# Turning heads and attention outputs in 32 x 32 blocks on VectorE and by way of DRAM, in the first transformer block

## The chip, the cores and the metric

The kernel runs on one core of a Trainium2 chip. The metric is device time in microseconds. A core has TensorE (PE; its weight loads are shown apart as PEld), VectorE (DVE), ScalarE (ACT), GpSimd (POOL) and SyncE (SP), which here only issues DMAs. Each engine and each queue works through its own list in order. Matrix products land in PSUM, which this part of the kernel uses as eight banks of 128 x 512 float32.

## The reference, cut to what matters

Two transformer blocks follow each other on `x` of 8 batches, 512 rows and 256 columns, all in float32. The change touches only the self attention of the first:

```python
h = modulate(ln(x), shift_sa, scale_sa)
q = ln(_heads(h, H)) * qn_w + qn_b        # 16 heads of 16 columns
k = ln(_heads(h, H)) * kn_w + kn_b
v = _heads(h, H)
attn = softmax(einsum('bhqd,bhkd->bhqk', q, k) * scale)
h = _unheads(einsum('bhqk,bhkd->bhqd', attn, v))
x = x + gate_sa[:, None, :] * h
```

After it the first block has cross attention over 64 context rows and a gated feed-forward layer. The second block has 64 columns a head and rotary positions.

## The kernel before, in words

`x` of a batch lies as 128 partitions by four row tiles (`NT`) by 256 columns. The first block handles one batch after another, and three stages of neighbouring batches are interleaved: `cycle(c)` issues self attention of batch `c` (`sa[c]`), the beginnings of that of `c + 1` (`nxt`), cross attention of `c - 1` (`x`, class `CrossAttention`) and feed-forward of `c - 2` and `c - 3` (`up`, `down`). `beginning()` does batch 0 and `ending()` what is left. The whole order is written by hand (`tc.manual_schedule` over all five engines): each engine issues in the order of the Python text. Which of the eight banks a `bank()` gets (line 75) is chosen by the framework when it builds the program.

The 16 heads are taken in four groups `g` of four heads. `c, par = divmod(g, 2)` picks a half of the columns (`zs[c]`) and even or odd heads, so that heads lie 32 partitions apart after a transpose.

- The heads' own normalisation: `centre` (DVE, L538 to L540), `square` (ACT, L544), `var` (DVE, L550, L551) and `scale` (POOL, the power L557 and the product L558) leave normed rows in `zs[c]`.
- `queries_keys(g)` transposes them: four 128 x 128 transposes on PE (L566) into a bank, then q and k on DVE out of that bank (L569, L570).
- `score(g, kt)` makes the scores of one tile of 128 keys, in four banks, one a head, four matmuls beside each other in the array; `exponentials` empties them on ACT (L615).
- `value(g, kt)` adds up the values of the four tiles of keys in one bank `o`, with the softmax denominators in a 17th column. After the last, ACT copies the bank to the tile `oT` (L591).
- `back(g)`, one group later, transposes `oT` by four PE transposes (L598) into a bank. DVE divides (L605 to L607) and checks (L129), POOL applies the gate and adds to `x` (L609, L610).

`group(scores, beside, short, values, rest)` sets the order of a group: two tiles' scores, `beside`, the other two tiles' scores, `short`, then the values. In a cycle group 0, 1, 2, one group of cross attention and group 3 follow each other. `short` of group 3 holds `nxt.queries_keys(0)`, `x.inverse(1)` (L687), `x.scaled(1)` (L691, L129), `nxt.var(1)` and `nxt.scale(1)`. In the steady cycles (3 to 6) `beside` of groups 0 and 1 ends with `blocks` of the feed-forward and of cross attention: `blocks_turned` (L413 to L418) turns 32 x 32 blocks of the normed rows on DVE, stores them to DRAM by four DMAs on SP and reads them back by one, so that `modulated` (ACT, L427) has them transposed. `spread` (L398) brings a row of gates or shifts to all partitions, on SP too. In cycle 1, `keys1` (matmuls, L868 and L869 on DVE, L873 and L874 on POOL) prepares keys for the second block, and after cycle 1 the feed-forward weights are loaded (L239).

Of the kernel before, what the change touches and what calls it, by code (L numbers as in the profile page):

```python
# [10 lines left out]
F32 = mybir.dt.float32  # L11
I32 = mybir.dt.int32
AF = mybir.ActivationFunctionType
ALU = mybir.AluOpType
# [30 lines left out]
def fast_path(ctx: ExitStack, tc: tile.TileContext, a: dict, out: bass.AP):  # L45

    nc = tc.nc
# [3 lines left out]
    small = ctx.enter_context(tc.tile_pool(name="small", bufs=4))  # L51
    dram = ctx.enter_context(tc.tile_pool(name="dram", bufs=2, space=bass.MemoryType.DRAM))
# [22 lines left out]
    def bank():  # L75
        return psum.tile([P, 512], F32, tag="bank", name="ps_B", bufs=8)
# [10 lines left out]
    def mm(o, lhsT, rhs, start=True, stop=True):  # L87
        nc.tensor.matmul(o, lhsT, rhs, start=start, stop=stop)  # L88


    ident = const.tile([P, P], F32, name="ident")
# [6 lines left out]
    rows = const.tile([P, 5 * D], F32, name="rows")  # L98
# [16 lines left out]
    def col(name):  # L115
        lo, hi = _COLS[name]
        return cols[:, lo:hi]
# [7 lines left out]
    def check(src):  # L125
        c = checks[0]
        checks[0] += 1
        for i, op in enumerate((ALU.max, ALU.min)):
            nc.vector.tensor_reduce(chk[:, i, c : c + 1], src, AX.X, op)  # L129
# [23 lines left out]

    def rstd_of(var, n, eps):

        r = small.tile([P, 64], F32, tag="rstd", name="rstd")
        nc.vector.tensor_scalar_add(r[:, :n], var, eps)  # L157
        nc.gpsimd.tensor_tensor(r[:, :n], r[:, :n], mhalf[:, :n], ALU.pow)  # L158
        return r
# [46 lines left out]
    qk_cols = keep0.tile([P, 2], F32, name="qk_cols")  # L206
# [3 lines left out]
    wk = sa0.enter_context(tc.tile_pool(name="sa0", bufs=2, side="right"))  # L210
# [3 lines left out]
    zs = [wk.tile([P, NT, DZ], F32, name=f"z{c}", bufs=1) for c in range(2)]  # L214
# [181 lines left out]
    def spread(dst, b, lo, n):  # L396

        nc.sync.dma_start(dst, modd[b : b + 1, lo : lo + n].to_broadcast([P, n]))  # L398
# [32 lines left out]
    def normed_in_pieces(pool, b, eps, take):  # L431

        def rows_():
            z = pool.tile([P, NT, D], F32, tag="z", name="z", bufs=1)
            take(z)
            return z

        return norm_pieces(rows_, xs[b], eps)
# [44 lines left out]
    class SelfAttention:  # L483
# [69 lines left out]
        def scale(self, c, par=None, eng=None):  # L553
# [3 lines left out]
            nc.gpsimd.tensor_tensor(var, var, half, ALU.pow)  # L557
            (eng or nc.gpsimd).tensor_tensor(z, z, var[:, :, :, None].to_broadcast([P, NT, n, HD0]), ALU.mult)  # L558

        def queries_keys(self, g):  # L560

            c, par = divmod(g, 2)
            ps = bank()
            lo = par * HD0
            for t in range(NT):
                nc.tensor.transpose(ps[:, t * P : (t + 1) * P], zs[c][:, t, lo : lo + P], ident)  # L566
            q = wk.tile([P, N], F32, tag="q", name="q", bufs=1)
            k = wk.tile([P, N], F32, tag="k", name="k", bufs=1)
            nc.vector.tensor_scalar(q, ps, qk_cols[:, 0:1], qk_cols[:, 1:2], ALU.mult, ALU.add)  # L569
            nc.vector.tensor_scalar(k, ps, col("kw"), col("kb"), ALU.mult, ALU.add)  # L570
            self.s[g] = (q, k)
# [9 lines left out]
        def value(self, g, kt):  # L581
            s = self.s
            c, par = divmod(g, 2)
            if kt == 0:
                s["o", g] = bank()
            for j in range(4):
                mm(s["o", g][32 * j : 32 * j + 32, :], s["h"][:, kt, 8 * c + 2 * j + par, :], s["p", kt][j],
                   kt == 0, kt == NT - 1)
            if kt == NT - 1:
                s["oT", g] = oT = wk.tile([P, N], F32, tag="oT", name="oT", bufs=1)  # L590
                nc.scalar.copy(oT, s["o", g])  # L591

        def back(self, g):
            b, s = self.b, self.s
            c, par = divmod(g, 2)
            ps = bank()
            for t in range(NT):
                nc.tensor.transpose(ps[:, t * P : (t + 1) * P], s["oT", g][:, t * P : (t + 1) * P], ident)  # L598
            attn = wk.tile([P, NT, 4, HD0], F32, tag="attn", name="attn", bufs=1)
            x, gate = (v.rearrange("p t (h d) -> p t h d", d=HD0)[:, :, 8 * c + par : 8 * c + 8 : 2]  # L600
                       for v in (xs[b], s["gate"][:, None, :]))
            i = ps.rearrange("p (t j e) -> p t j e", t=NT, j=4)
            inv = small.tile([P, NT, 4], F32, tag="inv", name="inv")
            den = small.tile([P, NT, 4], F32, tag="den", name="den")
            nc.vector.tensor_copy(den, i[:, :, :, HD0])  # L605
            nc.vector.reciprocal(inv, den)
            nc.vector.tensor_tensor(attn, i[:, :, :, 0:HD0], inv[:, :, :, None].to_broadcast([P, NT, 4, HD0]), ALU.mult)  # L607
            check(inv.rearrange("p t j -> p (t j)"))
            nc.gpsimd.tensor_tensor(attn, attn, gate.to_broadcast([P, NT, 4, HD0]), ALU.mult)  # L609
            nc.gpsimd.tensor_tensor(x, x, attn, ALU.add)  # L610
# [21 lines left out]
    class CrossAttention:  # L632
# [4 lines left out]
        def prepare(self, n):  # L637

            b, s = self.b, self.s
            if n == 0:  # L640
                s["gate"] = gate = wk2.tile([P, D], F32, tag="gate", name="gate", bufs=3)
                spread(gate, b, G_CA, D)
                s["pieces"] = normed_in_pieces(wk2, b, EPS0, lambda z: s.update(z=z))
            s["pieces"][n]()
            if n < 2:
                return
            gate = s["gate"]
            gb = wk2.tile([P, D], F32, tag="gb", name="gb", bufs=1)
            nc.gpsimd.tensor_tensor(gb, gate, row("cab0"), ALU.mult)
            add_row(b, gb)  # L650
# [96 lines left out]
    def group(scores, beside, short, values, rest=()):  # L747

        for fn in (*scores[:2], *beside, *scores[2:], *short, *values, *rest):
            fn()  # L750
# [50 lines left out]
    def cycle(c):  # L801

        s, nxt, prev = sa[c], of(sa, c + 1), sa[c - 1]
        x, done = ca[c - 1], of(ca, c - 2)
        up, down = of(ff, c - 2), of(ff, c - 3)
        keys = [lambda p=p: keys1(p) for p in range(NPAIR)] if c == 1 else [lambda: None] * NPAIR
        store = store_keys1 if c == 1 else lambda g: None
        late = [up.turn] if c == 2 else []
        soon, then = ([x.turn], []) if c == 1 else ([], [x.turn])
        rows2, rows3 = ([] if c < n else [s.blocks] for s, n in ((x, 2), (up, 3)))  # L810

        scores, values = of_self(s, 0)
        group(scores, [keys[0], keys[1], lambda: done.out(0), lambda: done.out(1), lambda: up.prepare(0), lambda: up.prepare(1),
                       lambda: down.down(0), lambda: up.prepare(2), *rows3],
              [lambda: s.queries_keys(1), lambda: prev.back(3), lambda: nxt.norm(0), lambda: nxt.norm(1)], values, late)
        scores, values = of_self(s, 1)
        group(scores, [keys[2], lambda: store(0), lambda: down.down(1), lambda: x.prepare(0), lambda: x.prepare(1),
                       *([up.turn] if c > 2 else []), lambda: up.up(0), lambda: x.prepare(2), keys[3], lambda: up.up(1), *rows2],
              [lambda: s.queries_keys(2), lambda: s.back(0), *soon, lambda: nxt.norm(2)], values)
        scores, values = of_self(s, 2)  # L820
        group(scores, [keys[4], *then, lambda: store(1), lambda: up.up(2), lambda: up.up(3), lambda: x.queries(0), lambda: x.queries(1)],
              [lambda: s.queries_keys(3), lambda: s.back(1), lambda: nxt.centre(0)], values)
        group([lambda: x.score(0), lambda: x.score(1)],
              [keys[5], lambda: nxt.square(0), lambda: up.up(4), keys[6], lambda: up.up(5), lambda: s.back(2), lambda: nxt.var(0),
               lambda: nxt.scale(0), lambda: nxt.centre(1)], [], [lambda: x.value(0), lambda: x.value(1)])
        scores, values = of_self(s, 3)
        group(scores, [keys[7], lambda: store(2), lambda: x.inverse(0), lambda: up.up(6), lambda: x.scaled(0), lambda: nxt.square(1),
                       lambda: up.up(7)],
              [lambda: nxt.queries_keys(0), lambda: x.inverse(1), lambda: x.scaled(1), lambda: nxt.var(1), lambda: nxt.scale(1)],
              values)  # L830
        store(3)
# [71 lines left out]
    wk2 = wk3 = w_1 = w_3 = w_2 = None  # L903
# [89 lines left out]
    with tc.tile_pool(name="ph4", bufs=2, reuse_waits="tile") as wk:  # L993
        NG = H // 4
        kb, vb = kv_first()
# [1334 lines left out]
```

## Time and profile before

| | us |
|---|---|
| median of 3 runs (2279.99 to 2281.34) | 2280.68 |
| the profiled execution's own time | 2284.83 |
| its span | 2282.9 |
| PE busy | 2258.7 |
| DVE busy | 1143.3 |
| ACT busy | 865.0 |
| POOL busy | 884.0 |
| one steady cycle of the first block (352.90 to 442.06) | 89.16 |

The first block takes about the first 740 us of the span, the second the rest. The line of an instruction is that of the listing above, except that all matmuls of the helper `mm` have L88; a matmul in float32 is recorded as two, a transpose as one. In a timeline row the columns are start, length from first to last instruction of the row, engine, line, operation, written tile and read tiles, and in brackets how long the engine sat idle before it and what ended that. In a row of windows they are the stretch, its length, each engine's busy time (and instructions), the granted PE clock, the DMA engines' busy share and GB/s. Normed heads are `z`, the value bank is a `ps_B` read into `oT`.

### The profile page before, as it was taken

To read this page: it belongs to the slowest core of one execution; us is meant where nothing else is said; L and a number is where in the kernel's file an instruction comes from. 1 tells how busy PE (TensorE), PEld (TensorE's weight loads), DVE (VectorE), ACT (ScalarE), POOL (GpSimd) and SP (SyncE) were. 2 spreads that over 40 slices of the span, in tenths; PEclk is the share of its full clock that TensorE was granted. 3 is DMA by queue.
4 is the path that set the end of the run, shared out by engine and by line. 5 is a ranking of instruction groups with operands and counts; after the bars stand their busy time and mean duration, and the time that the engine had idled before them with its cause. 6 is when DMAs were issued, how large, how long until landed. Compare 5 with 4: busy or idle time off the path is not lost.

```text
span 2282.9 us, 30663 instructions
## 1 busy us (share of the span) xinstructions
PE 2258.7 (99%) x12092; PEld 1139.7 (50%) x12092; DVE 1143.3 (50%) x1978; ACT 865.0 (38%) x1309; POOL 884.0 (39%) x552
## 2 busy tenths in 40 slices
PE   9999999999999999999999999999999999999999
PEld 4444554544545643535353534344445456567666
DVE  5676666665555345353544444444444566643220
ACT  4666555555542133242424243333342131321222
POOL 4653333333200056464645555555544333310110
PEclk9999999999999999999999999999999999999999
DMA  6120110101102001010101010111132445442221
GB/s 194 34 95 22 49 29 21 49 9 41 44 10 77 19 15 39 20 39 20 38 20 39 20 38 20 33 25 31 28 89 79 113 100 128 90 102 52 56 63 36
DMA packets 118119, 115.65 MB, mean 51 GB/s; under 512 B 37600, under 2 KB 91600, under 8 KB 117968
## 3 DMA queue, kind: packets, MB, share of 16 engines
q1 hardware_dynamic: 117104, 111.00, 19.0%
q8 instruction: 97, 1.59, 0.3%
q0 software_dynamic: 576, 2.10, 0.2%
q10 hardware_dynamic: 288, 0.52, 0.1%
q14 instruction: 54, 0.44, 0.1%
HBM read 85.73 MB, written 27.86 MB: 50 GB/s over the span
## 4 chain that ended last, share of the span: by engine, by line
PE 93%; DVE 2%; DMA 2%; POOL 1%; issue 1%; SPq 0%; ACT 0%; DVEq 0%; POOLq 0%; ACTq 0%
PE ps_P L88 41%; PE ps_B L88 30%; PE ps_X L88 7%; PE ps_S L88 6%; PE ps_D L88 5%; PE ps_O L88 3%; DMA rb<-rec 1%; PE ps_B L566 1%; POOL var L557 1%; PE ps_B L598 1%; DVE z L191 0%; DVE p L1337 0%; DMA rec<-rec 0%; DVE t L869 0%; DMA turned_d<-hT 0%
## 5 line engine op out<-in xcount | busy, mean ns | idle before, releaser
L615 ACT ACTIVATE p<-ps_B 128x512 f32<-128x512 f32 x576 | 290.9, 625 | 156.7 <-PE ps_B L88 156.7
L1060 ACT ACTIVATE p<-ps_P 128x1024 f32<-128x1024 f32 x256 | 244.8, 1025 | 87.6 <-PE ps_P L88 87.6
L88 PE MATMUL ps_P<-q,k 32*128 32x512 f32 x2048 | 238.9, 600 | 1.4 <-DVE t L1039 1.4
L1069 POOL TENSOR_TENSOR sm<-sm,p 128x1024 f32<-128x1024 f32 x64 | 177.5, 2774 | 134.8 <-ACT p L1060 134.1
L88 PE MATMUL ps_B<-hT,w 128*128 128x512 f32 x512 | 227.0, 597 | 1.3 <-ACT hT L407 0.9
L88 PE MATMUL ps_P<-p,v 128*32 128x512 f32 x2048 | 226.4, 594 | 0.0
L1028 ACT COPY v<-ps_P 128x1024 f32<-128x1024 f32 x32 | 32.4, 1012 | 377.1 <-PE ps_P L88 377.1
L1069 DVE TENSOR_TENSOR sm<-sm,p 128x1024 f32<-128x1024 f32 x64 | 102.7, 1605 | 144.4 <-ACT p L1060 144.4
L158 POOL TENSOR_TENSOR rstd<-rstd,mhalf 128x4 f32<-128x4 f32 x49 | 52.4, 1069 | 308.7 <-DVE rstd L157 307.5
L88 PEld LDWEIGHTS ps_P<-q,k 32*128 32x128 f32 x2048 | 99.1, 184 | 139.2 <-issue 113.6
L88 PEld LDWEIGHTS ps_B<-hT,w 128*128 128x128 f32 x512 | 95.3, 190 | 127.5 <-issue 97.0
L88 PEld LDWEIGHTS ps_P<-p,v 128*32 128x32 f32 x2048 | 63.3, 110 | 158.3 <-issue 134.0
L88 PE MATMUL ps_B<-q,k 16*128 16x512 f32 x1024 | 140.5, 618 | 1.2 <-DVE k L570 1.2
L1067 POOL TENSOR_TENSOR sm<-p 128x1024 f32<-128x1024 f32 x32 | 79.2, 2474 | 152.6 <-ACT p L1060 152.6
L1038 DVE TENSOR_TENSOR t<-ps_P,rope_c 128x1024 f32<-128x1024 f32 x64 | 78.4, 1225 | 106.7 <-POOL q L1042 64.5
L557 POOL TENSOR_TENSOR var<-var,mhalf 128x32 f32<-128x32 f32 (+1 forms) x17 | 88.0, 5174 | 105.4 <-DVE var L551 105.4
L1067 DVE TENSOR_TENSOR sm<-p 128x1024 f32<-128x1024 f32 x32 | 39.2, 1225 | 171.8 <-ACT p L1060 171.8
L88 PE MATMUL ps_P<-hT,w_sa_wq 128*128 128x512 f32 x256 | 118.4, 605 | 0.8 <-issue 0.8
L88 PE MATMUL ps_B<-p,h 128*32 128x512 f32 x1024 | 118.0, 599 | 0.0
L88 PE MATMUL ps_P<-hT,w_sa_wk 128*128 128x512 f32 x256 | 115.1, 592 | 0.0
L88 PE MATMUL ps_P<-w_sa_wv,hT 128*128 128x512 f32 x256 | 114.9, 592 | 0.0
L873 POOL TENSOR_TENSOR q<-t 128x512 f32<-128x512 f32 x36 | 46.2, 1283 | 177.0 <-DVE t L869 149.7
(245 smaller groups left out, 3660.8 us busy)
## 6 DMA issues: line engine op xcount, KB each, us to landing
z<-turned_d SPq DMA_DIRECT2D x35, 512.0 KB
rb<-rec_d SPq DMA_DIRECT2D x64, 256.0 KB
rb<-rec SPq DMA_DIRECT2D x32, 512.0 KB
turned_d<-hT SPq DMA_DIRECT2D x104, 128.0 KB
turned_d<-sm SPq DMA_DIRECT2D x36, 128.0 KB
out_dram<-x SPq DMA_DIRECT2D x15, 256.0 KB
x<-in_x_dram SPq DMA_DIRECT2D x7, 512.0 KB
gate<-modd SPq DMA_DIRECT2D x24, 128.0 KB
```

Of the source, the lines that this page charges most:

```text
L88: nc.tensor.matmul(o, lhsT, rhs, start=start, stop=stop)
L158: nc.gpsimd.tensor_tensor(r[:, :n], r[:, :n], mhalf[:, :n], ALU.pow)
L557: nc.gpsimd.tensor_tensor(var, var, half, ALU.pow)
L566: nc.tensor.transpose(ps[:, t * P : (t + 1) * P], zs[c][:, t, lo : lo + P], ident)
L598: nc.tensor.transpose(ps[:, t * P : (t + 1) * P], s["oT", g][:, t * P : (t + 1) * P], ident)
L615: nc.scalar.activation(p[i], ps, AF.Exp, scale=HD0 ** -0.5)
L873: nc.gpsimd.tensor_tensor(d[0], ec, os, ALU.subtract)
L1028: nc.scalar.copy(s["v", half][:, t0 : t0 + 2, :], ps)
L1038: nc.vector.tensor_tensor(c, ps, rope_c[:, None, :].to_broadcast([P, 2, N]), ALU.mult)
L1060: nc.scalar.activation(pr, pss[u], AF.Exp, scale=HD1 ** -0.5)
L1067: eng.tensor_tensor(s["sm", g, u], s["p", g, 0, u], s["p", g, 1, u], ALU.add)
L1069: eng.tensor_tensor(s["sm", g, u], s["sm", g, u], s["p", g, kt, u], ALU.add)
```

## The change

In batches 1 to 7 most of these transposes leave PE.

- `heads_turned(c)` is new. DVE turns the 32 x 32 blocks of `zs[c]` into a tile `zt`, four DMAs store it to DRAM, one reads 128 rows back over `zs[c]` (heads of even `g`) and one reads 112 rows into `zt` (odd `g`). `queries_keys` makes q and k from these tiles in SBUF. It is called for `c = 1` at the beginning of group 1's `beside` for the batch itself, and for `c = 0` of the next batch beside cross attention. Batch 0, and groups 0 and 1 of batch 1, keep the PE transposes.
- Where `by_blocks(g)` holds (all of batches 1 to 7 but the last group of batch 7), `value` ends with DVE turning the bank `o` into `oT`, four DMAs to DRAM and one back, in place of ACT's copy. `back` then reads `oT` in SBUF and issues no transpose.
- `centre(0)`, `square(0)`, `var(0)` and `scale(0)` of the next batch move from the cross attention's group to group 2.
- Two tiles get smaller: `rstd` from 64 columns to 4, and the gate of cross attention from three buffers to two.

```diff
+        def heads_turned(self, c):
+            zt = wk.tile([P, N], F32, tag="zt", name="zt", bufs=1)
+            z = zs[c][:, :, 0 : D // 2]
+            nc.vector.transpose(zt.rearrange("p (q t i) -> p t q i", q=4, t=NT), z.rearrange("p t (q j) -> p t q j", j=32))
+            d = dram.tile([4, 32, 4, P], F32, tag="heads", name="heads_d")
+            for r in range(4):
+                nc.sync.dma_start(d[:, :, r, :].rearrange("a j c -> j a c"),
+                                  zt[32 * r : 32 * r + 32].rearrange("j (a c) -> j a c", a=4))
+            d = d.rearrange("a j r c -> (a j) (r c)")
+            raw = zs[c].rearrange("p t d -> p (t d)")[:, 0:N]
+            nc.sync.dma_start(raw, d)
+            nc.sync.dma_start(zt[0 : P - HD0], d[HD0:P])
+            self.s["rows", 2 * c], self.s["rows", 2 * c + 1] = raw, zt[0 : P - HD0]
+
         def queries_keys(self, g):
             c, par = divmod(g, 2)
+            if ("rows", g) in self.s:
+                raw = self.s["rows", g]
+                n = raw.shape[0]
...
+                raw = raw.rearrange("p (r t i) -> p t r i", r=4, t=NT)
+                for o, w, b in ((q, qk_cols[0:n, 0:1], qk_cols[0:n, 1:2]), (k, col("kw")[0:n], col("kb")[0:n])):
+                    nc.vector.tensor_scalar(o[0:n].rearrange("p (t r i) -> p t r i", r=4, t=NT), raw, w, b, ALU.mult, ALU.add)
...
                 s["oT", g] = oT = wk.tile([P, N], F32, tag="oT", name="oT", bufs=1)
-                nc.scalar.copy(oT, s["o", g])
+                if self.by_blocks(g):
+                    nc.vector.transpose(oT.rearrange("p (r t d) -> p t r d", r=4, t=NT),
+                                        s["o", g].rearrange("p (t r i) -> p t r i", r=4, t=NT))
+                    d = dram.tile([4, 32, 4, P], F32, tag="back", name="back_d")
+                    for j in range(4):
+                        nc.sync.dma_start(d[:, :, j, :].rearrange("r i c -> i r c"),
+                                          oT[32 * j : 32 * j + 32].rearrange("i (r c) -> i r c", r=4))
+                    nc.sync.dma_start(oT, d.rearrange("r i j c -> (r i) (j c)"))
+                else:
+                    nc.scalar.copy(oT, s["o", g])
+
+        def by_blocks(self, g):
+            return self.b > 0 and (self.b, g) != (B - 1, 3)
 
         def back(self, g):
-            ps = bank()
-            for t in range(NT):
-                nc.tensor.transpose(ps[:, t * P : (t + 1) * P], s["oT", g][:, t * P : (t + 1) * P], ident)
+            if self.by_blocks(g):
+                i = s["oT", g].rearrange("p (j t e) -> p t j e", t=NT, j=4)
+            else:
+                ps = bank()
+                for t in range(NT):
+                    nc.tensor.transpose(ps[:, t * P : (t + 1) * P], s["oT", g][:, t * P : (t + 1) * P], ident)
+                i = ps.rearrange("p (t j e) -> p t j e", t=NT, j=4)
...
-        group(scores, [keys[2], lambda: store(0), lambda: down.down(1), lambda: x.prepare(0), lambda: x.prepare(1),
+        group(scores, [keys[2], lambda: store(0), lambda: s.heads_turned(1), lambda: down.down(1), lambda: x.prepare(0),
...
-              [lambda: s.queries_keys(3), lambda: s.back(1), lambda: nxt.centre(0)], values)
+        group(scores, [keys[4], *then, lambda: store(1), lambda: up.up(2), lambda: nxt.centre(0), lambda: up.up(3),
+                       lambda: nxt.square(0), lambda: x.queries(0), lambda: x.queries(1)],
+              [lambda: s.queries_keys(3), lambda: s.back(1), lambda: nxt.var(0), lambda: nxt.scale(0)], values)
         group([lambda: x.score(0), lambda: x.score(1)],
-              [keys[5], lambda: nxt.square(0), lambda: up.up(4), keys[6], lambda: up.up(5), lambda: s.back(2), lambda: nxt.var(0),
-               lambda: nxt.scale(0), lambda: nxt.centre(1)], [], [lambda: x.value(0), lambda: x.value(1)])
+              [keys[5], lambda: up.up(4), keys[6], lambda: up.up(5), lambda: s.back(2), lambda: nxt.heads_turned(0),
+               lambda: nxt.centre(1)], [], [lambda: x.value(0), lambda: x.value(1)])
```

More of the change, by code (lines that the diff above doesn't have):

```diff
@@ L154, in rstd_of @@
     def rstd_of(var, n, eps):
-        r = small.tile([P, 64], F32, tag="rstd", name="rstd")
+        r = small.tile([P, NT], F32, tag="rstd", name="rstd")
         nc.vector.tensor_scalar_add(r[:, :n], var, eps)
@@ L558, in scale @@
             (eng or nc.gpsimd).tensor_tensor(z, z, var[:, :, :, None].to_broadcast([P, NT, n, HD0]), ALU.mult)
+        def heads_turned(self, c):
[11 more added lines that the diff above has]
+            self.s["rows", 2 * c], self.s["rows", 2 * c + 1] = raw, zt[0 : P - HD0]
         def queries_keys(self, g):
             c, par = divmod(g, 2)
+            if ("rows", g) in self.s:
+                raw = self.s["rows", g]
+                n = raw.shape[0]
+                q = wk.tile([P, N], F32, tag="q", name="q", bufs=1)
+                k = wk.tile([P, N], F32, tag="k", name="k", bufs=1)
+                raw = raw.rearrange("p (r t i) -> p t r i", r=4, t=NT)
+                for o, w, b in ((q, qk_cols[0:n, 0:1], qk_cols[0:n, 1:2]), (k, col("kw")[0:n], col("kb")[0:n])):
+                    nc.vector.tensor_scalar(o[0:n].rearrange("p (t r i) -> p t r i", r=4, t=NT), raw, w, b, ALU.mult, ALU.add)
+                self.s[g] = (q, k)
+                return
             ps = bank()
@@ L601, in back @@
                        for v in (xs[b], s["gate"][:, None, :]))
-            i = ps.rearrange("p (t j e) -> p t j e", t=NT, j=4)
             inv = small.tile([P, NT, 4], F32, tag="inv", name="inv")
@@ L640, in prepare @@
             if n == 0:
-                s["gate"] = gate = wk2.tile([P, D], F32, tag="gate", name="gate", bufs=3)
+                s["gate"] = gate = wk2.tile([P, D], F32, tag="gate", name="gate")
                 spread(gate, b, G_CA, D)
@@ L816, in cycle @@
         scores, values = of_self(s, 1)
-        group(scores, [keys[2], lambda: store(0), lambda: down.down(1), lambda: x.prepare(0), lambda: x.prepare(1),
-                       *([up.turn] if c > 2 else []), lambda: up.up(0), lambda: x.prepare(2), keys[3], lambda: up.up(1), *rows2],
+        group(scores, [keys[2], lambda: store(0), lambda: s.heads_turned(1), lambda: down.down(1), lambda: x.prepare(0),
+                       lambda: x.prepare(1), *([up.turn] if c > 2 else []), lambda: up.up(0), lambda: x.prepare(2), keys[3],
+                       lambda: up.up(1), *rows2],
               [lambda: s.queries_keys(2), lambda: s.back(0), *soon, lambda: nxt.norm(2)], values)
         scores, values = of_self(s, 2)
-        group(scores, [keys[4], *then, lambda: store(1), lambda: up.up(2), lambda: up.up(3), lambda: x.queries(0), lambda: x.queries(1)],
-              [lambda: s.queries_keys(3), lambda: s.back(1), lambda: nxt.centre(0)], values)
+        group(scores, [keys[4], *then, lambda: store(1), lambda: up.up(2), lambda: nxt.centre(0), lambda: up.up(3),
+                       lambda: nxt.square(0), lambda: x.queries(0), lambda: x.queries(1)],
+              [lambda: s.queries_keys(3), lambda: s.back(1), lambda: nxt.var(0), lambda: nxt.scale(0)], values)
         group([lambda: x.score(0), lambda: x.score(1)],
-              [keys[5], lambda: nxt.square(0), lambda: up.up(4), keys[6], lambda: up.up(5), lambda: s.back(2), lambda: nxt.var(0),
-               lambda: nxt.scale(0), lambda: nxt.centre(1)], [], [lambda: x.value(0), lambda: x.value(1)])
+              [keys[5], lambda: up.up(4), keys[6], lambda: up.up(5), lambda: s.back(2), lambda: nxt.heads_turned(0),
+               lambda: nxt.centre(1)], [], [lambda: x.value(0), lambda: x.value(1)])
         scores, values = of_self(s, 3)
```

## The prediction, made before the result was known

> **What bounds the kernel now.** First the page's busy list, its chain, and the windows of two steady cycles of the first block (one cycle is what `cycle(c)` issues).
>
> ```profile
> PE 2258.7 (99%) x12092; PEld 1139.7 (50%) x12092; DVE 1143.3 (50%) x1978; ACT 865.0 (38%) x1309; POOL 884.0 (39%) x552
> PE 93%; DVE 2%; DMA 2%; POOL 1%; issue 1%; SPq 0%; ACT 0%; DVEq 0%; POOLq 0%; ACTq 0%
> 352.90:442.06 89.16, 89.16 (x492) 44.71 (x496) 55.55 (x114) 49.40 (x95) 29.58 (x19) 1.00 0.12 32
> ```
>
> TensorE is the chain, and in a steady cycle it is busy for all of the 89.16 us; DVE has 33 us to spare. So removing PE work looks like pure gain. But a busy PE is not a PE at its peak, so next I read the PE and ACT timelines at the end of a group of heads.
>
> ```profile
> 368.82 2.03 PE L88 MATMUL ps_B<-q,k 16*128 16x512 f32 x16
> 370.79 0.66 PE L566 MATMUL ps_B<-ident,z 128*128 128x128 f32 x4
> 371.28 0.60 PE L598 MATMUL ps_B<-ident,oT 128*128 128x128 f32 x4
> 371.81 3.64 PE L88 MATMUL ps_B<-p,h 128*32 128x512 f32 x32
> 375.38 2.00 PE L88 MATMUL ps_B<-q,kb 32*128 32x512 f32 x16
> 370.04 4.03 ACT L615 ACTIVATE p<-ps_B 128x512 f32<-128x512 f32 x8 [5.66 <-PE ps_B L88]
> ```
>
> Two sets of four transposes take 371.81 - 370.79 = 1.02 us, 0.128 each. But ACT's eight exponentials end at 374.07, and the last quarter of the values (3.57 / 4 = 0.89 each) needs the last of them: the transposes lie almost wholly in the shadow of ACT. Last, the DVE timeline where one cycle gives way to the next, with ACT's copy there.
>
> ```profile
> 400.61 0.81 DVE L569 TENSOR_SCALAR q<-ps_B,qk_cols 128x512 f32<-128x512 f32 x1 [1.80 <-PE ps_B L566]
> 402.06 3.34 DVE L687 RECIPROCAL den<-den 128x512 f32<-128x512 f32 x1
> 407.94 0.18 DVE L551 TENSOR_SCALAR var<-var 128x32 f32<-128x32 f32 x1
> 408.03 0.69 DVE L471 TENSOR_TENSOR tmp<-ps_B,gate 128x512 f32<-128x512 f32 x1
> ...
> 404.07 2.00 PE L88 MATMUL ps_B<-q,k 16*128 16x512 f32 x16
> 404.29 0.59 ACT L591 COPY oT<-ps_B 128x512 f32<-128x512 f32 x1 [1.62 <-PE ps_B L88]
> 405.29 2.06 ACT L615 ACTIVATE p<-ps_B 128x512 f32<-128x512 f32 x4 [0.42 <-PE ps_B L88]
> ```
>
> DVE is not free there until 408.03, while the value bank `o` is emptied by ACT at 404.88, in time for the next scores. This decides my forecast.
>
> **What is removed.** `heads_turned` serves 26 sets of queries and keys (two in block 1, four in blocks 2 to 7), `by_blocks` 27 outputs: 53 sets of four transposes. At 0.128 each the ceiling is 212 x 0.128 = 27 us. What a cycle really gains goes by the last exponential. From it (374.07) to the next scores at least 0.89 + 0.22 = 1.11 us remain, 0.22 for waking PE and filling it (from 375.38 less 371.81 and four quarters of 0.86, plus 0.1). Group 2: 375.18 instead of 375.38, gain 0.20. Group 1 (exponentials end at 355.06): 356.17 against 356.40, 0.23. Group 0 (421.73): 422.84 against 423.08, 0.24. Group 3 (402.67): 403.78 against 404.07, 0.29. Only the set of `back(2)` beside cross attention (384.28 to 384.81) is free of ACT: 0.53. Together 1.5 us of the 4.2 that a cycle spends on them (3 x 1.02 + 0.59 + 0.53).
>
> **What is added on DVE.** The turning of 128x512 was not in the trace: half of L413's 1.24 for 128x1024 is 0.62, a read of ps of that size (L569) 0.81; I take 0.70, nearest to DVE's other 128x512 reads of ps (L471, 0.69). Six of them a cycle, 4.2 us, less some 0.15 on each of eight q and k (SBUF, L691: 0.69, instead of 0.81 from ps): DVE's sum goes up by 3, which does not matter. Its order does. `value` now ends with the turning on DVE, queued behind everything of `short`, where ACT's copy stood behind nothing; and until it ends the bank stays taken. The eight next scores want eight banks and there are eight.
>
> Cycle to cycle: q can start when the scores have been read, about 0.5 earlier (400.1); q and k 1.25; the rest up to 408.03 is 5.97: DVE is free at 407.3, the bank at 408.0. The scores, now from 403.78, want their eighth bank about 0.95 later (404.73). They may instead take the bank of the first exponential, ready 1.22 (404.07 to 405.29) + 0.59 + 0.15 = 1.96 after their start, 405.74. The trace says that banks are not dealt in turn: in cycle 1 the bank of a late key (read by L869 until 105.28) was left alone by the scores and given to the later L406. So I take 405.74: 1.0 us of new idleness, net of the 0.29 +0.74 against before.
>
> Group 0 to 1: DVE ended `norm(1)` at 424.98; without PE's transposes q is not earlier, since L413 ends at 420.66, and q and k are 0.2 shorter: turning until 425.5. The scores from 422.84 want it at 423.8; the first exponential gives 424.8: net +0.80. Group 1 to 2: q starts 0.5 earlier, L191 (444.09, 2.34) ends at about 445.8, turning until 446.5, wanted at 446.3: net +0.07. Group 2: turning follows the values directly, 0.15 + 0.70, about in time: -0.06. `back(2)`: -0.53. Sum **+1.0 us a cycle**, for cycles 2 to 6: +5.1. Cycle 7 has no next block's norms and keeps ACT's copy at its end: -0.7.
>
> **What is added on SP.** Per cycle 2 x 6 + 4 x 5 = 32 DMAs, 0.62 each to issue (four: 2.56, L416), 20 us of an otherwise idle queue; about 3.5 MB more at 89 us a cycle, 40 GB/s, beside the window's 32. What counts is order: each read waits 2.07 for its four writes (423.24 to 425.31), so a turn takes about 5 us of SP and some 8 to land. SP in group 1: `blocks`' read 425.31, two spreads, `back(0)` 426.7 to 432, `heads_turned(1)` to 437.5, landed at about 441; q wants it at 441.7. Tight, hidden; 1 us more only moves DVE, and 3.5 us more stops PE. `heads_turned(0)` (DVE at 386, landed 394.5, wanted 400) and `back(3)` (408 to 416, wanted 421.8) have room. ACT loses 27 copies of 0.59, none on the path.
>
> Moving `centre(0)` to `scale(0)` a group ahead costs nothing in a steady cycle: POOL's power (L557, 5.47) starts near 375.5, after `back(1)`, instead of 387.66, and is done before DVE turns the heads at 386; DVE's 1.6 us for `centre(0)` fall between `up(2)` and `up(3)`, where it sat idle 0.8 and more. If that cover went, DVE would be late by those 1.6 us at the next banks. The smaller rstd and the third gate buffer cost nothing either: a gate is read for the last time in group 0, before the next but one is spread.
>
> Cycles 1 and 2 have less cover. The gate of `x.prepare(0)`, spread at 93.25 before, now waits behind `back(0)` and `heads_turned(1)`, until about 105.8, landed at 108; POOL's L649, at 102.24 before, and behind it L448, the ropes and `norm(2)` go 5.7 late until POOL's idle 6.02 before 122.33 takes it up. `centre(0)`, moved ahead, waits for that and holds the banks of `x.queries`. I charge 0.5 (group 0), 1.0 (group 1) and 1.2 (two banks, one exponential each): +2.7. The feed-forward weights, issued at 137, 144 and 151, now come after `back(3)`, at about 157; w_3 is there at about 165.5 and wanted at 164.43 + 2.7: hidden. The next `heads_turned(1)` queues behind w_2: +1.0. Bounds: 0 if POOL's and DVE's slack takes all of it, 8 if w_3 is on the path.
>
> **The clock.** After PE sat idle 0.97 before 140.80 it ran at half speed for 3.4 us:
>
> ```profile
> 140.80 1.11 PE L566 MATMUL ps_B<-ident,z 128*128 128x128 f32 x4 [0.97 <-POOL z L558]
> 140.20:143.60 3.40, 2.80 (x16) 1.16 (x20) 3.37 (x4) 1.77 (x4) 3.40 (x3) 0.50 0.40 165
> ```
>
> That is 1.7 us lost each time; the wait of some 0.6 us that every steady cycle has in its last scores (397.38 to 399.91, 2.53 instead of 1.93) never did it. A dozen new waits of about 0.8 to 1.0 lie between: 0 to 12 x 1.7 = 20 us; I take one or two, +2.5. [...]
>
> [...]
>
> **Sum.** 5.1 - 0.7 + 2.7 + 1.0 + 2.5 = +10.6, against the profiled execution's 2284.83 us (span 2282.9). That execution is 4.2 above the median of 2280.68; the same step from the median gives **2291**.
>
> **Rivals.** (a) *The scores wait for the value bank itself.* For: before, the eighth score did take the bank ACT had just emptied. Against: the late key's bank. Price: 3.2 instead of 0.74 at five cycle ends, 1.6 instead of 0.8 at five first groups, +16: 2307, more with the clock. (b) *Faster: the new wait isn't there*, because the bank is emptied by about 404.7 or another is idle; it decides at the cycle ends. Then 1.5 a cycle over six cycles: -9, 2271.5. For: PE is 93% of the chain. Against: DVE's row at 408.03. Were ACT no shadow either, -27: 2254. (c) *The DRAM trip becomes the bound:* `heads_turned(1)` lands after 445; each microsecond beyond costs six; two make 2303. (d) *Losses and gains cancel:* clock and cycles 1 and 2 cost nothing, +4.4 at most.
>
> **How the numbers follow.** Forecast 0.42, (a) 0.19, (c) 0.05, (b) 0.18, (d) 0.16. No change means within 0.2%, 4.6 us, about what a measurement of this kernel can tell. Faster 0.18, same 0.16, slower 0.66. The range goes down to (b), 2271, and up past (a) with three half-clock stretches, 2312; the forecast's own is 2285 to 2300.
>
> **What would show it.** L566 and L598 fall to 24 and 20 matmuls. The group ends: PE idle of about 1 us in the scores after the values, put down to ACT L615 or to the new transpose; values that wait for `p`. Cycles of about 90.2 us instead of 89.16. POOL's L649 near 108. Half-clock stretches between 170 and 640. I am wrong if cycles are shorter than 88.5 (no bank wait), or if q waits for a DMA.

## The result and the profile after

The changed kernel takes 2306.1 us (median of 4 runs, 2298.72 to 2307.5), the kernel before beside it 2281.01: a ratio of 1.010, interval 1.0082 to 1.0117. It is slower, as forecast, but by 25 us and not by 10.6. The profiled execution took 2307.33 us (span 2305.5), 22.5 more than that of before (2284.83); its trace is taken apart below.

From here on line numbers are those of the changed kernel: q and k out of the turned heads are L585, DVE's turning of the heads L564 and of the outputs L617, the transposes still on PE L591 and L638, the exponentials L655, the gate's product on POOL L689, the queries of cross attention L703. In some of the experiments' kernels they stand one or two lines further down.

First the page's busy list, and the group of the scores' matmuls (last column: idle time of PE just before them, and who ended it).

```profile
PE 2269.9 (98%) x11880; PEld 1130.7 (49%) x11880; DVE 1161.9 (50%) x2018; ACT 849.9 (37%) x1282; POOL 883.2 (38%) x552
L88 PE MATMUL ps_B<-q,k 16*128 16x512 f32 x1024 | 156.1, 620 | 11.8 <-DVE oT L617 10.4 <-DVE k L585 0.7 <-DVE k L595 0.5
```

PE issues 212 instructions fewer and is busy for 11 us more: much of its "busy" is waiting inside a row of scores or a lower clock. A new name stands behind the scores, the turning of the outputs on DVE. The same group before:

```profile
L88 PE MATMUL ps_B<-q,k 16*128 16x512 f32 x1024 | 140.5, 618 | 1.2 <-DVE k L570 1.2
```

Next the windows of two steady cycles (the number behind POOL's is the granted clock).

```profile
426.23:517.88 91.65, 91.14 (x457) 43.67 (x457) 57.02 (x120) 47.06 (x91) 29.63 (x19) 0.98 0.28 70
517.88:607.97 90.09, 89.58 (x457) 42.48 (x457) 57.40 (x120) 47.14 (x91) 29.63 (x19) 1.00 0.27 72
```

The second, at full clock, is the forecast's cycle: 90.09 against 89.17, +0.92. The first has one stretch of 3.41 us at half speed (from 447.4) and is 1.56 longer. Now the place where one cycle gives way to the next, from the timelines of PE, DVE and ACT:

```profile
423.31 2.99 PE L88 MATMUL ps_B<-q,k 16*128 16x512 f32 x16
426.23 3.72 PE L88 MATMUL ps_B<-w_o,oT 128*128 128x256 f32 x16
...
427.09 0.72 DVE L617 STREAM_TRANSPOSE oT<-ps_B 128x512 f32<-128x512 f32 x1 [0.35 <-issue]
...
424.53 4.03 ACT L655 ACTIVATE p<-ps_B 128x512 f32<-128x512 f32 x8 [2.25 <-PE ps_B L88]
```

The scores take 2.99 us where they took 2.00 (the row of 404.07 before). They end at 426.23, before DVE has even begun to turn the value bank (427.09): the eighth bank came from the first exponential (424.53), as forecast. Between groups 0 and 1 it is otherwise:

```profile
443.00 1.99 PE L88 MATMUL ps_B<-q,k 16*128 16x512 f32 x14
445.51 1.12 PE L88 MATMUL ps_B<-q,k 16*128 16x512 f32 x2 [0.51 <-DVE oT L617]
...
444.74 0.72 DVE L617 STREAM_TRANSPOSE oT<-ps_B 128x512 f32<-128x512 f32 x1
...
444.22 4.03 ACT L655 ACTIVATE p<-ps_B 128x512 f32<-128x512 f32 x8 [2.25 <-PE ps_B L88]
```

Here the first of the eight exponentials was done by about 444.8 (444.22 + 4.03 / 8 and a little), but the last two matmuls start only at 445.51, when the turning has ended (444.74 + 0.72): these scores wait for the value bank itself. From the first to the last they take 3.63 us; before, the same scores took 2.00 (from 423.08).

The largest single loss is in cycle 1, again from the timelines of PE, DVE, POOL and SP:

```profile
108.98 1.99 PE L88 MATMUL ps_B<-q,k 16*128 16x512 f32 x14
115.99 2.07 PE L88 MATMUL ps_B<-q,k 16*128 16x512 f32 x2 [5.02 <-DVE oT L617]
...
107.78 0.55 DVE L585 TENSOR_SCALAR q<-z,qk_cols 128x512 f32<-128x512 f32 x1 [1.92 <-DMA z<-heads_d]
109.69 5.63 DVE L191 TENSOR_SCALAR ln<-x,mv,rstd 128x256 f32<-128x256 f32 x4
115.23 0.70 DVE L617 STREAM_TRANSPOSE oT<-ps_B 128x512 f32<-128x512 f32 x1
...
109.34 0.86 POOL L689 TENSOR_TENSOR gb<-gate,rows 128x256 f32<-128x256 f32 x1 [6.09 <-DMA gate<-modd]
110.28 2.34 POOL L448 TENSOR_TENSOR x<-x,gb 128x1024 f32<-128x1024 f32 x1
...
104.89 0.34 SPq L571 DMA_DIRECT2D z<-heads_d  x1
105.74 0.43 SPq L398 DMA_DIRECT2D gate<-modd  x1
```

The same normalisations and the gate's product before:

```profile
107.62 3.25 DVE L191 TENSOR_SCALAR ln<-x,mv,rstd 128x256 f32<-128x256 f32 x4
102.24 0.72 POOL L649 TENSOR_TENSOR gb<-gate,rows 128x256 f32<-128x256 f32 x1
```

Read the rows after from the bottom up. SP issues the gate's spread at 105.74, behind the turned heads. POOL, 6.09 us idle for it, starts at 109.34 (before: 102.24), and its products then run beside DVE's four normalisations L191, which take 5.63 us instead of 3.25. DVE was late already, as q waited 1.92 us for the turned heads. The turning of the value bank stands behind all this, and PE for 5.02 us.

**Where 22.3 us went** up to the end of cycle 7 (starts of PE's matmuls against those of before; a cycle begins with the first matmul of cross attention's output product, `w_o`; little changes behind it):

| stretch | forecast | measured | how it is worked out |
|---|---|---|---|
| up to 106 us | 0 | -0.9 | shift of the values' start |
| cycle 1 from there | +2.7 | +8.3 | shift from -0.9 to +7.4 at 155.58; some 2 of it are half clock: 7.12 us of PE's work at half speed from 112.87 to 123.11, 2.84 from 140.23 before, half of each lost |
| steady part of cycles 2 to 6 | +5.1 | +4.6 | 5 x 0.92, the cycle at full clock |
| more in cycle 2 | +1.0 | +2.1 | 87.31 - 79.45 - 0.92, less three half-clock stretches at 1.6 |
| cycle 7 | -0.7 | -1.35 | 85.42 against 86.77 |
| half clock, cycles 2 to 5 | +2.5 | +9.5 | three stretches in cycle 2 at 1.6; 4.7 over 0.92 each in cycles 3 to 5 |

The steady cycle, on which the prediction spent its working, held. Cycle 1 (5.6 too little) and the clock (7 too little) did not; with its 2 us in cycle 1 the clock is the largest item, about half of the 22. In cycle 2 PE waits 1.70 and 1.65 us for the value bank behind groups 0 and 1, where a steady cycle waits 0.51 us and not at all.

### The profile page after: what moved, and what is told of

Its sections match the earlier page's. It is cut to its first block, busy times and chain, and to the rows that moved or that the text cites. A ratio compares the mean times of both kernels' runs of the same rounds, so it can differ in the third digit from the quotient of the medians.

```text
span 2305.5 us, 30615 instructions
## 1 busy us (share of the span) xinstructions
PE 2269.9 (98%) x11880; PEld 1130.7 (49%) x11880; DVE 1161.9 (50%) x2018; ACT 849.9 (37%) x1282; POOL 883.2 (38%) x552
## 3 DMA queue, kind: packets, MB, share of 16 engines
q8 instruction: 95, 1.56, 0.3%
## 4 chain that ended last, share of the span: by engine, by line
PE 91%; DVE 4%; DMA 3%; issue 1%; POOL 1%; SPq 1%; ACT 0%; DVEq 0%; POOLq 0%; ACTq 0%
PE ps_P L88 41%; PE ps_B L88 30%; PE ps_X L88 7%; PE ps_S L88 6%; PE ps_D L88 5%; PE ps_O L88 3%; DMA rb<-rec 1%; DMA turned_d<-hT 1%; DMA rec<-rec 0%; DVE p L1379 0%; DVE z L191 0%; DVE ln L191 0%; POOL var L557 0%; DVE t L911 0%; DVE hT L413 0%
## 5 line engine op out<-in xcount | busy, mean ns | idle before, releaser
L655 ACT ACTIVATE p<-ps_B 128x512 f32<-128x512 f32 x576 | 290.6, 629 | 201.9 <-PE ps_B L88 201.8
L88 PE MATMUL ps_B<-q,k 16*128 16x512 f32 x1024 | 156.1, 620 | 11.8 <-DVE oT L617 10.4
L88 PE MATMUL ps_B<-p,h 128*32 128x512 f32 x1024 | 131.7, 596 | 0.0
L88 PE MATMUL ps_B<-w,hid 128*128 128x256 f32 x512 | 118.2, 391 | 0.0
```

The source lines that it names most:

```text
L655: nc.scalar.activation(p[i], ps, AF.Exp, scale=HD0 ** -0.5)
```

## The experiments

The theory after the result: the loss is the value bank, held by an engine that comes to it late. Rivals: the trips through DRAM (SP's queue, late landings), and for cycles 1 and 2 the late gate. All ratios are to the kernel before, on the same chip.

**Heads alone.** Outputs keep ACT's copy and the PE transposes.

```diff
         def by_blocks(self, g):
-            return self.b > 0 and (self.b, g) != (B - 1, 3)
+            return False
```

> Heads turned by blocks as in the change, outputs as before (ACT empties the value bank, PE transposes). Bank theory (VectorE's late turning keeps the value bank and PE waits for it): the waits of 1.0 at the end of each cycle and 1.6 after group 0, the 5.0 in cycle 1 and the half-clock stretches after them are gone, only the small gains of 0.2 to 0.3 a group ahead of the exponentials stay: about 2276 us, 30 below the changed kernel. DRAM theory (the trips by way of DRAM are late in cycles 1 and 2): q still waits for its rows and GpSimd for the gate, some 8 us lost before 200 us of the span: about 2288.

Measured 2281.15 us, 0.9991 (0.9982 to 1.0): the loss is gone, but there is little gain, and the time lies between the two forecasts. The window of a steady cycle at full clock shows one, 89.17 - 87.77 = 1.40 us:

```profile
404.77:492.54 87.77, 87.77 (x476) 43.57 (x473) 54.45 (x116) 49.47 (x95) 29.60 (x19) 1.00 0.19 50
```

Cycle 1 gives it back. The DVE and POOL timelines have the late gate and the slow L191 without any turned output:

```profile
101.72 0.55 DVE L585 TENSOR_SCALAR q<-z,qk_cols 128x512 f32<-128x512 f32 x1 [0.58 <-DMA z<-heads_d]
103.63 5.34 DVE L191 TENSOR_SCALAR ln<-x,mv,rstd 128x256 f32<-128x256 f32 x4
...
102.98 0.74 POOL L689 TENSOR_TENSOR gb<-gate,rows 128x256 f32<-128x256 f32 x1 [4.45 <-DMA gate<-modd]
```

POOL's `h` is late in turn, and `centre(0)` and the queries of cross attention behind it: PE waits 3.35 us for q of L703 in this cycle. So the bank theory was right about the steady cycles, and the DRAM theory about cycle 1.

**Outputs alone.** The heads stay on PE.

```diff
         def heads_turned(self, c):
+            return
```

> Outputs turned by blocks as in the change, heads' rows transposed on PE as before. Bank theory: the waits for the value bank stay in every cycle (1.0 and 1.6), with half-clock stretches of 1.7 each after some of them, without the 5.0 in cycle 1, whose lateness began with the rows: about 2296 us. DRAM theory: SyncE's queue is short again, the loss of cycles 1 and 2 (15 of the 22 us) goes: about 2286.

Measured 2307.64 us, 1.0105 (1.0089 to 1.012). The outputs alone cost as much as the whole change, so the 2296 of the theory was too low: the steady cycle is 91.97, +2.8. The likely reason, not tested by itself: q again waits for PE's transposes of the heads, and the turning stands behind q. In the PE timeline, between groups 0 and 1:

```profile
440.66 1.99 PE L88 MATMUL ps_B<-q,k 16*128 16x512 f32 x14
443.63 1.12 PE L88 MATMUL ps_B<-q,k 16*128 16x512 f32 x2 [0.98 <-DVE oT L618]
```

**ACT empties the bank.** The whole change, with every DMA and every turning; but ACT copies the bank to a tile in SBUF as before, and DVE turns that.

```diff
                 if self.by_blocks(g):
+                    o = wk.tile([P, N], F32, tag="oc", name="oc", bufs=1)
+                    nc.scalar.copy(o, s["o", g])
                     nc.vector.transpose(oT.rearrange("p (r t d) -> p t r d", r=4, t=NT),
-                                        s["o", g].rearrange("p (t r i) -> p t r i", r=4, t=NT))
+                                        o.rearrange("p (t r i) -> p t r i", r=4, t=NT))
...
-        p = [wk.tile([P, N], F32, tag="p", name="p", bufs=14) for _ in pss]
+        p = [wk.tile([P, N], F32, tag="p", name="p", bufs=13) for _ in pss]
```

> The whole change, but ACT copies the value bank to a tile in SBUF as before and VectorE turns that tile (the exponentials' tiles are 13 instead of 14 to make room). Bank theory: no wait for the bank anywhere, few half-clock stretches, a steady cycle of about 87.7 us (89.16 less 0.2 to 0.3 in four groups and 0.5 beside cross attention): 2268 to 2276 us, faster than before by some 7. DRAM theory: rows and gate are as late in cycles 1 and 2 as in the changed kernel, 2290 us or more. If the new waits came from the turning's time on VectorE and not from the bank: no change, 2305.

Measured 2282.64 us, 0.9999 (0.9989 to 1.001): 23 us of the whole change's loss are back, with DRAM trips, DVE's work and all DMAs in place. So it is the held bank that cost them, and the rivals' 2290 and 2305 are both missed. But the trips are not free. The gain of 2268 to 2276 did not come either: cycle 1 again loses to the gate (L191 5.58 us, PE 4.05 us idle for the queries of cross attention), and in cycle 2 q waits 4.82 us for its turned heads. PE is idle for 1.55 us behind that, a half-clock stretch follows, and the cycle takes 82.61 us instead of 79.45 (3.16 more: the wait, and 1.61 for the stretch). The row on DVE:

```profile
185.15 0.55 DVE L585 TENSOR_SCALAR q<-z,qk_cols 128x512 f32<-128x512 f32 x1 [4.82 <-DMA z<-heads_d]
```

The steady cycle tells what turning is worth once no bank is held:

```profile
498.33:585.68 87.35, 87.35 (x460) 42.53 (x456) 58.02 (x120) 49.41 (x95) 29.60 (x19) 1.00 0.28 74
```

1.82 us for eight sets of transposes a cycle, 0.42 more than the heads alone: the outputs' sets lie in ACT's shadow but for the one beside cross attention.

**The whole change from batch 3 on.**

```diff
         def heads_turned(self, c):
+            if self.b < 3:
+                return
...
-            return self.b > 0 and (self.b, g) != (B - 1, 3)
+            return self.b > 2 and (self.b, g) != (B - 1, 3)
```

> The whole change, but only from batch 3 on; batches 1 and 2 keep the transposes on PE. My reading of the changed trace (15 of 22 us are lost in cycles 1 and 2, then 0.8 to 1.0 a cycle and a half-clock stretch of 1.7 in every second or third): about 2288 us. Rival (the loss lies evenly in the cycles): 2281 + 22 x 4 / 6, about 2296.

Measured 2290.59 us, 1.0036 (1.0023 to 1.0049). With cycles 1 and 2 spared, 15 of the 25 us are gone, and nearer my 2288 than the rival's 2296. The moved `centre(0)` to `scale(0)` stay moved in all cycles here, and from the values of cycle 1's group 1 to the end of cycle 2 PE falls back by 0.5 us in all: that move costs next to nothing by itself.

**The gate first.** The whole change with one entry moved.

```diff
-        group(scores, [keys[2], lambda: store(0), lambda: s.heads_turned(1), lambda: down.down(1), lambda: x.prepare(0),
-                       lambda: x.prepare(1), *([up.turn] if c > 2 else []), lambda: up.up(0), lambda: x.prepare(2), keys[3],
+        group(scores, [keys[2], lambda: store(0), lambda: down.down(1), lambda: x.prepare(0),
+                       lambda: s.heads_turned(1), lambda: x.prepare(1), *([up.turn] if c > 2 else []), lambda: up.up(0), lambda: x.prepare(2), keys[3],
```

> The whole change, but in group 1 heads_turned(1) is issued behind x.prepare(0) instead of ahead of down.down(1), so that SP issues the gate's spread before the turned heads' six DMAs. Theory (in cycle 1 the late gate makes POOL late, and POOL then slows DVE's L191 and holds centre(0) with the banks of x.queries): the gate's product L689, at 109.34 in the trace after, starts near 104, L191 there falls from 5.63 towards 3.3, and of the some 9 us that cycles 1 and 2 lose to this 3 to 5 come back: 2301 to 2303 us. Rival (cycles 1 and 2 lose through the value bank alone): 2306, no change, and the extra 0.58 wait of q for its DMA grows instead.

Measured 2302.68 us, 1.0093 (1.0078 to 1.0109): 3.4 us below the whole change's median, but in ratio 1.0093 against 1.010, with intervals that overlap, so no gain is shown. The timelines of cycle 1 say what became of it:

```profile
107.75 1.13 DVE L585 TENSOR_SCALAR q<-z,qk_cols 128x512 f32<-128x512 f32 x1 [1.69 <-DMA z<-heads_d]
108.81 1.50 DVE L585 TENSOR_SCALAR k<-z,cols 128x512 f32<-128x512 f32 x1
111.21 2.33 DVE L191 TENSOR_SCALAR ln<-x,mv,rstd 128x256 f32<-128x256 f32 x4
...
107.33 1.27 POOL L915 TENSOR_TENSOR q<-t 128x512 f32<-128x512 f32 x1
108.56 1.46 POOL L916 TENSOR_TENSOR q<-t 128x512 f32<-128x512 f32 x1
...
114.22 1.12 PE L88 MATMUL ps_B<-q,k 16*128 16x512 f32 x2 [1.36 <-DVE oT L617]
```

POOL is in time, L191 is fast (2.33), and PE's wait falls from 5.02 to 1.36. But q still waits for the turned heads, and now q and k run beside POOL and take 1.13 and 1.50 instead of 0.55. By PE's starts against before, from the values near 106 us to cross attention, cycle 1 loses 5.1 us instead of 8.8. The later cycles give part of it back: one at full clock takes 90.43 us instead of 90.09.

**Heads alone, gate first.** The same move, and outputs as before:

```diff
-            return self.b > 0 and (self.b, g) != (B - 1, 3)
+            return False
```

> Only the heads are turned, for all batches from 1 on, and SP issues the gate's spread ahead of heads_turned(1). Theory (late gate): the 6 to 7 us that cycles 1 and 2 lost with heads only shrink to 1 to 3, the gain of 1.87 a steady cycle stays: 2275 to 2277 us. Rival (the heads' own trip is late in the first cycles): no better than with the heads first, 2281, with q waiting longer than 0.58 for its DMA in cycle 1.

Measured 2280.19 us, 0.9991 (0.9981 to 1.0), the same as heads alone. My 2275 to 2277 was wrong, and the rival's time and its sign came: in cycle 1 q waits 1.75 us for its DMA instead of 0.58. The theory was right in part, for by the measure above cycle 1 loses 4.7 us instead of 7.7 (3.2 and 3.4 of them at half clock). But the steady cycle takes it back, 88.36 instead of 87.77: behind `x.prepare(0)` DVE turns the heads only at 435.28, and the scores before the next values take 2.77 us instead of 2.06. (The 1.87 us a cycle that this expectation and the next two count on is too much: the windows show 1.40.)

```profile
407.07:495.43 88.36, 88.36 (x476) 43.68 (x472) 54.31 (x116) 49.53 (x95) 29.59 (x19) 1.00 0.19 49
```

So in cycle 1 SP's queue makes one of the two late, whichever is second (with the heads first POOL waits 4.45 us for the gate, with the gate first q waits 1.75 us for the heads), and there is no slack for either.

**Heads alone, from batch 3 and from batch 2 on.** Outputs as before (`by_blocks` returns False), and for the first kernel

```diff
         def heads_turned(self, c):
+            if self.b < 3:
+                return
```

with 2 in place of 3 for the second.

> Only the heads are turned by DVE, and only from batch 3 on; all outputs go by ACT's copy and PE, as before. Theory (the heads' turning saves 1.87 us in each steady cycle, and what the first kernel with heads only lost again it lost in cycles 1 and 2 alone): 4 cycles x 1.87 and some 0.5 of cycle 2 and 1 of cycle 7, about -8 to -9 against before: 2273 to 2274 us. Rival (the loss of the first cycles only moves to where the turning begins, in cycles 2 and 3): 2278 to 2282.

> Only the heads are turned by DVE, from batch 2 on (with heads from batch 3 on: 0.9971 of before). Theory (what is lost is lost in cycle 1, where the heads of batch 1 are turned and q waits for them; cycle 2 gains as the others do): one cycle of 1.87 us more than from batch 3 on, 2275 us. Rival (the loss comes in whichever cycle is first, or in cycle 2, whose weights queue behind the heads' DMAs): 2278 to 2281.

Measured 2277.06 us, 0.9971 (0.996 to 0.9981), and 2275.49, 0.9968 (0.9955 to 0.998): faster than before, by about what the steady cycle promises (four or five cycles of 1.4). The first is 3 us above its forecast of 2273 to 2274, which had counted 1.87 a cycle; the second met its 2275. Where the heads' loss sits is plain from PE's starts against before: from the values near 106 us to cross attention of cycle 1 it falls back by 7.7 us with heads from batch 1 on (3.4 of them in a half-clock stretch, 117.75 to 124.58) and by 1.0 from batch 2 on, while the next cycle, cross attention to cross attention, takes 75.9 in both (76.76 before). The loss belongs to the batch whose heads are turned in cycle 1, and does not move with the beginning. The difference between the two kernels is within the intervals.

**Outputs of groups 1 and 2 alone.**

```diff
         def heads_turned(self, c):
+            return
...
-            return self.b > 0 and (self.b, g) != (B - 1, 3)
+            return self.b > 0 and g in (1, 2)
```

> Outputs alone, of groups 1 and 2, batches 1 to 7; no heads turned, and groups 0 and 3 keep ACT's copy (all outputs: 1.0105 of before, with scores of 4.02 us behind group 0's values, 2.92 behind group 1's and group 3's, instead of 1.93). Theory (the loss is the bank held behind the values of groups 0 and 3): per cycle +1.0 behind group 1, less 0.53 for the set beside cross attention, nothing else: +3, and some 2 more in cycle 1: 2285 us. Rival (the load on DVE, SP and DRAM as such): two thirds or a half of what all outputs cost, 2294 to 2298.

Measured 2279.19 us, 0.9993 (0.9984 to 1.0002). Against all outputs (1.0105) that is 1.1%, or 26 us: half of the turnings, and none of the loss. Load on DVE, SP or DRAM as such would have cost about half. It is also 6 us less than my 2285. In the PE timeline the scores behind group 1's values wait a little (2.68 instead of 2.00), those behind group 3's do not:

```profile
351.77 2.68 PE L88 MATMUL ps_B<-q,k 16*128 16x512 f32 x16
...
399.40 2.00 PE L88 MATMUL ps_B<-q,k 16*128 16x512 f32 x16
```

The set that is spared beside cross attention (0.44) makes up for that, and the cycle stays at 89.13.

**Heads from batch 2 on, and the outputs of group 2.**

```diff
         def heads_turned(self, c):
+            if self.b < 2:
+                return
...
-            return self.b > 0 and (self.b, g) != (B - 1, 3)
+            return self.b > 1 and g == 2
```

> Heads from batch 2 on as in the kernel beside it, and the outputs of group 2 alone by DVE, whose value bank nobody waits for in the trace after, and whose set of four transposes, beside cross attention, is the only one that no exponential hides. Theory (what counts is in which group the bank is held): 0.53 us gained in each of six cycles, 3 us below the kernel beside it: 2272 us. Rival (any output by way of DVE and DRAM costs, in its bank or its trip): the same as the kernel beside it or slower, 2275 to 2280.

Measured 2273.68 us, 0.9965 (0.9951 to 0.9978), the best of all: 0.35% below the kernel before. Its cycle takes 87.34 to 87.43 where heads alone take 87.78, as one set of four matmuls less beside cross attention should bring; in the runs this 0.4 us a cycle does not stand out from the kernel without it.

```profile
397.36:484.70 87.34, 87.34 (x472) 43.07 (x468) 55.12 (x117) 48.81 (x94) 29.56 (x19) 1.00 0.21 56
```

## Why the prediction was right in sign and wrong in size

**What is removed.** Right: more than half of the removed transposes' time lay in ACT's shadow. Of 4.2 us a cycle 1.5 were forecast as the gain; 1.82 came once no bank was held, 1.40 of it with the heads alone. For `back(2)` 0.53 was forecast and 0.44 came.

**What is added on DVE.** The sizes were right: turning takes 0.72 (L617) and 0.69 (L564), forecast 0.70, and q and k out of SBUF 0.55 where I had 0.66. Which bank the scores take was half right. From cycle to cycle it is the first exponential's; net of the values' earlier start that cost +0.51 (forecast +0.74). From group 0 to 1 it is the value bank's own: scores +1.62, net +1.31 (forecast +0.80). In place of one rule for all groups, as I had it and as rival (a) had it, each place has its own bank. Groups 1 and 2 came out 0.2 better each than forecast (-0.16 for +0.07, -0.29 for -0.06, by the shifts of PE's starts in the cycle at full clock), so the sum of the cycle, +1.0 for a measured +0.92, owes something to errors that cancel.

**What is added on SP, steady cycles.** Right: no q waits for a DMA there, the core moves 70 to 72 GB/s where the estimate was 72, and moving `centre(0)` costs nothing. SP needs some 14 us a cycle for the new DMAs and not 20 (four stores take 1.8, a read 0.34 to 0.43), which changes nothing. With `heads_turned(1)` behind one more piece 0.6 us a cycle were lost, but not through the trip: q does not wait for its DMA there either, and what moved is the order on DVE.

**Cycle 1: the first step that failed.** I saw the late gate and put POOL's product of the gate (L649 before, L689 now) near 108 (109.34 came), and I charged 2.7 for what follows: 8.3 came, some 2 of it half clock. Two things were missing. The heads' trip itself is late in cycle 1 (q waits 1.92), which I had looked at only in the steady cycle. (In cycle 2 it is late again, by 0.69 us.) And POOL was shifted as if it could run at any time, while beside it DVE's L191 takes 2.4 us longer. Both stand ahead of the one instruction that empties the value bank, and there they add up to PE's wait of 5.02 us. The kernels with the gate first show both: L191 is fast there, and q waits again.

**The clock: the second, mis-sized, 2.5 for 9.5.** This term is off by more than any other. The price of a stretch, 1.7, was about right (1.56 between the two cycles shown). The count was not: I took one or two of a dozen waits, and six came in cycles 2 to 5. The steady wait that I leaned on, which never did it, was a poor guide to waits that come on top of it. And the row of 140.80 was read too simply: half speed begins at 140.23, while that wait of 0.97 us still lasts. Why six came and not two stays open.

**The rivals.** The time of (a), 2307, is what was measured, but not by its mechanism: the trace has none of its waits for the value bank at the cycle ends, which were most of its 16 us, and those held neither clock nor cycle 1. That the time agrees is luck. Its wait behind the first groups did come, at a net 1.31 for its 1.6. (c) did not occur in the steady cycles. (b), no bank wait, is the steady cycle of the kernel in which ACT empties the bank, with 1.82 gained for its 1.5, but cycles 1 and 2 used the gain up. (d) did not come.

## What to carry to other kernels

Before work is taken off the bounding engine, look for what hides it: the sets were worth 4.2 us a cycle by count, and 1.8 when all were gone and nothing else was lost. And ask of each PSUM bank who empties it, in what place of that engine's list: an instruction of 0.7 us on an engine half idle cost 1% because it stood behind others. A change that suits the steady state should be looked at again in the first cycles, where other work shares its queues; here the best kernel begins it one batch later and turns the outputs of group 2 alone, and even so it gains only 0.35%.

## What the runs showed of the hardware that was not expected

**DVE slows down beside POOL, in some forms only.** A single L191 (float32, SBUF to SBUF) takes 0.41 us while POOL is idle (103.61 in the changed kernel) and 2.50 beside POOL's L448 (110.27 to 112.77; L448 runs from 110.28 to 112.62). So four of them took 5.63 us in cycle 1, and 2.33 in the kernel with the gate first, where only the short L649 and L650 of POOL (0.72 and 0.73) ran beside two of them; q and k (L585) took 1.13 and 1.50 instead of 0.55. The ropes on DVE, which read one operand from PSUM, did not slow down: L911 took 0.68 at 105.39 in the kernel with the gate first, beside POOL's L448 (105.01 to 107.37), and 0.68 at 105.18 in the changed kernel, where POOL was idle. In the changed kernel each of those four L191 ends 0.15 us after the instruction of POOL beside it (at 110.35, 112.77, 114.04 and 115.31, where L689 ends at 110.20, L448 at 112.62, L915 at 113.89 and L916 at 115.16). What stretches them is not shown: no run here tells one cause from another.

**The clock falls behind some short waits, and not only there.** The record of the clock in the changed kernel's trace has stretches at half speed (granted 0.50), of 3.413 us or two or three times that, which begin at whole multiples of 3.413 us from each other (51.4, 82.2, 112.9 and so on up to 447.4, 116 of them after the first). PE is not idle ahead of each of them: in the 3.41 us before 447.4 PE shows 2.90 us of matmuls, and in those before 51.4, 82.2 and 334.7 it shows as busy throughout. The trace of before has a stretch at 51.5 too and that of heads alone none, though the kernels do the same work up to there. And the same wait between groups 0 and 1, 1.62 us long, had a stretch behind it in cycles 3 and 5 and none in cycles 4 and 6. What decides is not settled: all that the runs show is that kernels with fewer such waits had less of it (mean granted clock 0.988 to 0.991 in the runs of the whole change, 0.989 to 0.993 with outputs alone, 0.993 to 0.997 before, 0.994 to 0.997 with the outputs of groups 1 and 2). Up to 760 us, in one trace of each, the stretches add up to 44 us in the whole change, 31 with outputs alone, 17 before, 10 with the outputs of groups 1 and 2 and 10 in the best kernel.
